# Transposing by VectorE blocks and a detour through DRAM in a two-layer attention kernel

## The chip, the cores and the metric

The kernel runs on one core of one Trainium2 chip. The core has five engines that run side by side, each with its own queue of instructions: TensorE (PE, matrix products; PEld is its weight load), VectorE (DVE), ScalarE (ACT), GpSimd (POOL) and SyncE (SP), which in this kernel issues every DMA. An engine takes its instructions strictly in the order the build has given it, and waits on semaphores for what other engines or DMAs deliver. The metric is the time of one launch on the device in microseconds, as the median of several runs; beside it stands one profiled execution with a trace of every instruction.

## What is computed

Four images of 128 channels and 64 x 64 pixels (4096 tokens) go through two layers. The reference, cut to what matters:

```python
# layer 0, channels first
g = _gn(x)                                            # group norm
v, gate = split(sigmoid(conv_bn(g, Wvg, svg, bvg)))
q = conv_bn(g, Wq, sq, bq) * 64**-0.5; k = conv_bn(g, Wk, sk, bk)
attn = softmax(q.T @ k)
x = x + conv_bn((v @ attn.T) * gate, Wp, sp, bp)
# layer 1, tokens first
t = to_tokens(x)
h = _ln_t(t); q = h @ W1
t = t + softmax(q @ q.T) @ h                          # symmetric scores
f = batch_norm(_ln_t(t) @ W2.T)
t = t + scan over tokens of y = sigmoid(f_t + y @ V.T)
x = from_tokens(t, x)
```

All data is 32-bit float. Layer 0 works with channels on the 128 partitions, the layer norms need tokens on the partitions, and the products after them need channels again. So tiles of 128 x 512 are turned over several times for each block of 512 tokens.

## The kernel before

Each image is handled alone, in a loop over `b`: group norm (`group_norm`), the projections q, k, v and gate (`project`), attention of layer 0 (`layer0`), attention of layer 1 (`layer1`). After the fourth image comes the token scan.

**Layer 0.** Eight blocks `n` of 512 queries. For each block 16 pairs of key tiles: two score products into `ps` (L186), the exponential on ScalarE into one of five buffers `e` (L189), the running sum of `e` on VectorE (`acc`, L198), and the weighted sums `o` (L326). When a block is done, `finish` puts five steps into the list `pending`, and the loop takes one of them out after every second pair of the next block, so that they fall between the products of that block: `sums` (the denominators), `residual` (four transposes of the input `xb` by TensorE, L351, and a copy on ScalarE), `tokens` (the output projection straight into token order, four products of 128 columns, L357; the sum with the residual; layer norm into `h`), `turn` (four transposes of `h` by TensorE, L372, and a copy), `queries` (the product with layer 1's weight into `qt`, L377). The steps of the last block have no next block to hide in: `flush` runs them one after the other, and layer 1 begins with the `qt` that they make.

**Layer 1.** The scores are symmetric, so only the blocks (n, a) with a <= n are computed (L502, exponential L508). Each tile `e` with a < n is used twice: as it is (`direct`, L404), and turned over (`reversed_products`, L417). To turn it over, VectorE transposes it in 32 x 32 blocks into `dd` (L513), and 16 DMAs of 64 KB move the blocks to where they belong in `tt` (L532), SBUF to SBUF. There are 28 such turned tiles for each image, two buffers `dd` and three buffers `tt`; a turned tile is due four steps of the loop after it was made. The row sums of a turned tile are taken by VectorE (L422) and its product is added to `oacc` (L429). When the last turned tile of a block is done, `finish` puts four steps into `pending`: `tokens` (four transposes of `oacc` by TensorE, L456, sum with `t`, layer norm into `h2`), `result` (four transposes of `t`, L467, a copy, one store of 256 KB to `t2_d`, L470), `turn` (four transposes of `h2`, L475, a copy into `th`), `inputs` (the product `mw`, L480, its statistics, and a copy into `wxs`). Blocks run from n = 7 down to 0, so the blocks get shorter towards the end of an image, and the steps of the last blocks fall into the next image's `project`, or after the fourth image into a bare `flush`.

A step's work is written into the code at the place where it is taken out of `pending`; the build then orders the instructions of each engine's queue, and this order is fixed when the kernel runs. SP's queue holds the loads of `x`, the stores and loads of `t_d`, the 16 DMAs of each turned tile and the stores of the result, all in one line: an entry that waits holds everything behind it.

Of the kernel before, what the change touches and what calls it, by code (L numbers as in the profile page):

```python
# [9 lines left out]
F32 = mybir.dt.float32  # L10
# [7 lines left out]
P = 128  # L18
B, C, N = 4, 128, 4096
# [3 lines left out]
NT = N // P  # L23
# [5 lines left out]
QB = 512  # L29
NB = N // QB  # L30
NQ = QB // P
# [17 lines left out]
def conv_attn_hybrid_kernel(  # L49
# [8 lines left out]
    nc = tc.nc  # L58
# [5 lines left out]
    t_d = dram.tile([B, NB, P, NQ, C], F32, name="t_d")  # L64
# [43 lines left out]
    def inv_sqrt(dst, var, eps):  # L108
# [6 lines left out]
        tc, x, out, t_d, t2_d,  # L115
# [21 lines left out]
def fast(  # L137
    tc, x, out, t_d, t2_d, wt, col, par, bpc, bc, ident, gavg, ones, shift, inv_sqrt, par_ok
):
    nc = tc.nc  # L140
# [7 lines left out]
    with ExitStack() as st:  # L148
# [10 lines left out]
        pending: deque = deque()  # L159

# [60 lines left out]

        def layernorm(src, dst):

            mv = stat.tile([P, NQ, 2], F32, tag="mv", name="mv")
            rstd = stat.tile([P, NQ], F32, tag="rstd", name="rstd")
            for j in range(NQ):
                s6 = stat.tile([P, 6], F32, tag="s6", name="s6")
                nc.vector.bn_stats(s6, src[:, j, :])  # L228
                nc.vector.bn_aggr(mv[:, j, :], s6)  # L229
            inv_sqrt(rstd, mv[:, :, 1], EPS_LN)  # L230
            for j in range(NQ):
                nc.vector.tensor_scalar(  # L232
                    dst[:, j, :], src[:, j, :], mv[:, j, 0:1], rstd[:, j : j + 1],
                    ALU.subtract, ALU.mult,
                )

# [74 lines left out]
        def layer0(b, gate, q, k, v):  # L311
# [20 lines left out]
            def finish(n, o, acc):  # L332
                cs, ts = bass.ts(n, QB), bass.ts(n, NQ)
                og = work.tile([P, QB], F32, tag="og", name="og")
                nc.scalar.copy(og, o[1])
                nc.vector.tensor_tensor(og, o[0], og, ALU.add)
                nc.vector.tensor_tensor(og, og, gate[:, cs], ALU.mult)
                rinv = stat.tile([P, NQ], F32, tag="rinv", name="rinv")
                xb = work.tile([P, QB], F32, tag="xb", name="xb", bufs=2)
                t = work.tile([P, NQ, C], F32, tag="t", name="t", bufs=2)  # L340
                ht = work.tile([P, QB], F32, tag="th", name="ht")
                nc.sync.dma_start(xb, x[b, :, cs])
                nc.gpsimd.tensor_scalar(xb, xb, bpc, None, ALU.add)  # L343

                def sums():
                    denominators(acc, b * NT + n * NQ, rinv)

                def residual():
                    m = ps_m.tile([P, NQ, P], F32, tag="m", name="mx")
                    for j in range(NQ):  # L350
                        nc.tensor.transpose(m[:, j, :], xb[:, bass.ts(j, P)], ident)  # L351
                    nc.scalar.copy(t, m)

                def tokens():
                    m = ps_m.tile([P, NQ, P], F32, tag="m", name="mt")
                    for j in range(NQ):
                        nc.tensor.matmul(  # L357
                            m[:, j, :], lhsT=og[:, bass.ts(j, P)], rhs=wt["ps"],
                            start=True, stop=True,
                        )  # L360
                    for j in range(NQ):
                        nc.vector.scalar_tensor_tensor(
                            t[:, j, :], m[:, j, :], rinv[:, j : j + 1], t[:, j, :],
                            ALU.mult, ALU.add,
                        )
                    nc.sync.dma_start(t_d[b, n], t)
                    layernorm(t, h[:, ts, :])

                def turn():
                    m = ps_m.tile([P, QB], F32, tag="m", name="mh")  # L370
                    for j in range(NQ):
                        nc.tensor.transpose(m[:, bass.ts(j, P)], h[:, n * NQ + j, :], ident)  # L372
                    nc.scalar.copy(ht, m)

                def queries():
                    m = ps_m.tile([P, QB], F32, tag="m", name="mq")
                    nc.tensor.matmul(m, lhsT=wt["a"], rhs=ht, start=True, stop=True)  # L377
# [7 lines left out]
        def layer1(b, h, qt):  # L385
# [55 lines left out]
            def finish(n):  # L441
                cs = bass.ts(n, QB)
                rinv = stat.tile([P, NQ], F32, tag="rinv", name="rinv")
                t = work.tile([P, NQ, C], F32, tag="t", name="t1", bufs=2)
                h2 = work.tile([P, NQ, C], F32, tag="h2", name="h2")
                th = work.tile([P, QB], F32, tag="th", name="th")
                nc.sync.dma_start(t, t_d[b, n])

                def tokens():
# [4 lines left out]
                    m = ps_m.tile([P, NQ, P], F32, tag="m", name="mt")  # L454
                    for j in range(NQ):
                        nc.tensor.transpose(m[:, j, :], oacc[:, n, bass.ts(j, P)], ident)  # L456
# [5 lines left out]
                    layernorm(t, h2)  # L462

                def result():
                    m = ps_m.tile([P, QB], F32, tag="m", name="mr")
                    for j in range(NQ):
                        nc.tensor.transpose(m[:, bass.ts(j, P)], t[:, j, :], ident)  # L467
                    t2 = work.tile([P, QB], F32, tag="xb", name="t2", bufs=2)
                    nc.scalar.copy(t2, m)
                    nc.sync.dma_start(t2_d[b, :, cs], t2)  # L470

                def turn():
                    m = ps_m.tile([P, QB], F32, tag="m", name="mh")
                    for j in range(NQ):
                        nc.tensor.transpose(m[:, bass.ts(j, P)], h2[:, j, :], ident)  # L475
                    nc.scalar.copy(th, m)

                def inputs():
                    m = ps_m.tile([P, QB], F32, tag="m", name="mw")
                    nc.tensor.matmul(m, lhsT=wt["f"], rhs=th, start=True, stop=True)  # L480
# [6 lines left out]
                pending.extend([tokens, result, turn, inputs])  # L487

            for n in range(NB - 1, -1, -1):
                o = None  # L490
                for a in range(n, -1, -1):
# [37 lines left out]
                    if a < n:  # L529
                        for p in range(NQ):  # L530
                            for f in range(NQ):
                                nc.sync.dma_start(  # L532
                                    t[bass.ts(f, 32), p], d[bass.ts(p, 32), f]
                                )
                        turned.append((clock + 4, n, a, t))
# [14 lines left out]
        ok = stat.tile([P, 2, 2 * B * NT], F32, tag="ok", name="ok", bufs=1)  # L550
# [490 lines left out]
```

## Time and profile before

| | us |
|---|---|
| median of 3 runs | 3354.91 (3354.78 to 3356.2) |
| the profiled execution, its own time | 3355.76 |
| its span, first to last instruction | 3353.9 |

| row of the profile | busy us | one takes, ns |
|---|---|---|
| PE, layer 0 products `o` (L326) | 960.1 | 590 |
| PE, layer 0 scores `ps` (L186) | 539.5 | 608 |
| PE, layer 1 scores (L502) | 547.3 | 604 |
| PE, layer 1 direct products (L404) | 527.7 | 592 |
| PE, layer 1 turned products (L417) | 402.8 | 592 |
| ACT, layer 0 exponential (L189) | 521.0 | 1024 |
| ACT, layer 1 exponential (L508) | 391.2 | 683 |
| DVE, layer 0 running sums (L198) | 548.7 | 1225 |
| DVE, row sums of turned tiles (L422) | 252.9 | 2258 |

A row gives the code line, the engine, the instruction, output and input. Matrix instructions overlap in the pipeline, so busy time divided by the count is less than the duration of one. A 32-bit product appears as two instructions, a transpose as one. The granted TensorE clock was 0.972 over the span. DMA engines moved 179.24 MB, 53 GB/s in the mean.

### The profile page before, as it was taken

The page shows a single profiled execution, that of the slowest core. Times are in us where ns is not written, and L with a number is a line of the kernel's source. Part 1 is how long each engine was busy: PE and PEld are TensorE (multiplying, and loading weights), DVE is VectorE, ACT ScalarE, POOL GpSimd, SP SyncE. Part 2 cuts the span into 40 slices and gives each one's busy share as a digit, 9 for nine tenths or more (in the row PEclk, how much of TensorE's full clock was granted, in tenths as well). Part 3 has the DMA queues.
Part 4 walks back from the last instruction along what each step waited for, and adds up shares of the span by engine and source line. Part 5 has one row for each costly group of instructions (what it writes and reads, how often), then busy time and mean ns, then how long its engine had stood idle before and what let it go on. Part 6 is the DMA issues. An engine that isn't in the chain of part 4 may idle for free.

```text
span 3353.9 us, 32409 instructions
## 1 busy us (share of the span) xinstructions
PE 3148.9 (94%) x11210; PEld 1437.9 (43%) x11210; DVE 1708.3 (51%) x2793; ACT 1171.5 (35%) x2050; POOL 144.1 (4%) x183
## 2 busy tenths in 40 slices
PE   6999999997899999999699999999979999999976
PEld 3444444443444444444344444444434444444433
DVE  4545544555555544555645554455555555345556
ACT  3443432332434333233244343323233444332324
POOL 0000000000000000000000000000000000000000
PEclk9999999998999999999899999999989999999998
DMA  1000023332000003333200001333300000233334
GB/s 41 13 10 10 10 70 90 92 91 88 10 10 13 13 13 88 91 90 92 67 7 13 13 7 35 90 95 93 102 26 13 7 13 10 63 91 92 91 97 175
DMA packets 109084, 179.24 MB, mean 53 GB/s; under 512 B 31472, under 2 KB 31984, under 8 KB 107888
## 3 DMA queue, kind: packets, MB, share of 16 engines
q1 hardware_dynamic: 108912, 177.08, 19.4%
q8 instruction: 92, 1.51, 0.2%
q14 instruction: 80, 0.66, 0.1%
HBM read 34.35 MB, written 25.17 MB: 18 GB/s over the span
## 4 chain that ended last, share of the span: by engine, by line
PE 88%; DVE 6%; ACT 2%; POOL 1%; issue 1%; DMA 1%; SPq 0%; DVEq 0%; POOLq 0%; ACTq 0%
PE o L326 26%; PE ps L186 14%; PE ps L502 14%; PE o L404 14%; PE ot L417 11%; PE mq L377 1%; PE pvg L293 1%; PE mt L357 1%; POOL rstd L111 1%; PE md L214 1%; PE mw L480 1%; PE pvg L297 1%; DMA xg<-in_x_dram 1%; DVE t L458 1%; DVE s L228 1%
## 5 line engine op out<-in xcount | busy, mean ns | idle before, releaser
L326 PE MATMUL o<-e,v 64*128 64x512 f32 x4096 | 960.1, 590 | 0.0
L198 DVE TENSOR_TENSOR acc<-acc,e 128x1024 f32<-128x1024 f32 x448 | 548.7, 1225 | 525.3 <-ACT e L189 519.5
L189 ACT ACTIVATE e<-ps 128x1024 f32<-128x1024 f32 x512 | 521.0, 1024 | 684.5 <-PE ps L186 684.5
L508 ACT ACTIVATE e<-ps,shift 128x512 f32<-128x512 f32 x576 | 391.2, 683 | 940.1 <-PE ps L502 768.3
L326 PEld LDWEIGHTS o<-e,v 64*128 64x128 f32 x4096 | 397.3, 188 | 486.6 <-issue 479.0
L502 PE MATMUL ps<-qt 128*128 128x512 f32 x1152 | 547.3, 604 | 2.7 <-ACT qt L378 2.7
L186 PE MATMUL ps<-q,k 64*128 64x512 f32 x2048 | 539.5, 608 | 9.0 <-ACT e L189 4.8
L404 PE MATMUL o<-e,h 128*128 128x512 f32 x1152 | 527.7, 592 | 0.0
L417 PE MATMUL ot<-tt,h 128*128 128x512 f32 x896 | 402.8, 592 | 0.0
L513 DVE STREAM_TRANSPOSE dd<-e 128x512 f32<-128x512 f32 x448 | 285.7, 683 | 125.1 <-ACT e L508 82.4
L502 PEld LDWEIGHTS ps<-qt 128*128 128x128 f32 x1152 | 217.6, 194 | 269.9 <-issue 240.0
L404 PEld LDWEIGHTS o<-e,h 128*128 128x128 f32 x1152 | 217.1, 191 | 260.2 <-issue 260.2
L186 PEld LDWEIGHTS ps<-q,k 64*128 64x128 f32 x2048 | 185.6, 187 | 223.1 <-issue 123.2
L417 PEld LDWEIGHTS ot<-tt,h 128*128 128x128 f32 x896 | 170.2, 190 | 214.3 <-issue 212.4
L422 DVE TENSOR_REDUCE slots<-tt 128x4 f32<-128x2048 f32 x112 | 252.9, 2258 | 2.3 <-DMA tt<-dd 1.7
L429 DVE TENSOR_TENSOR oacc<-oacc,ot 128x512 f32<-128x512 f32 x84 | 57.4, 684 | 309.7 <-PE ot L417 309.7
L232 DVE TENSOR_SCALAR h<-t,mv,rstd 128x128 f32<-128x128 f32 x256 | 73.0, 346 | 94.5 <-POOL rstd L111 94.4
L508 ACT ACTIVATION_READ_ACCUMULATOR e<-ps,shift 128x1 f32 x576 | 113.0, 196 | 0.0
L343 POOL TENSOR_SCALAR xb<-xb,bpc 128x512 f32<-128x512 f32 x32 | 57.0, 1781 | 1112.4 <-DMA xb<-in_x_dram 1112.4
L110 POOL TENSOR_SCALAR rstd<-mv 128x4 f32<-128x4 f32 x64 | 14.6, 229 | 1949.0 <-DVE mv L229 1949.0
L427 DVE COPY oacc<-ot 128x512 f32<-128x512 f32 x28 | 19.4, 692 | 139.5 <-PE ot L417 139.5
L293 PE MATMUL pvg<-w_vs,xg 128*128 128x128 f32 x256 | 42.7, 318 | 31.9 <-ACT xg L304 23.8
(112 smaller groups left out, 1510.9 us busy)
## 6 DMA issues: line engine op xcount, KB each, us to landing
tt<-dd SPq DMA_DIRECT2D x1792, 64.0 KB, 2.0
t_d<-t SPq DMA_DIRECT2D x64, 256.0 KB, 2.0
xg<-in_x_dram SPq DMA_DIRECT2D x16, 512.0 KB, 5.6
xb<-in_x_dram SPq DMA_DIRECT2D x32, 256.0 KB, 2.7
t<-t_d SPq DMA_DIRECT2D x32, 256.0 KB, 2.7
t2s<-t_d SPq DMA_DIRECT2D x4, 2048.0 KB, 14.8
out_dram<-t2s SPq DMA_DIRECT2D x4, 2048.0 KB, 15.6
w<-in_wts_dram SPq DMA_DIRECT2D x1, 512.0 KB, 3.5
```

The costliest lines, as they stand in the source:

```text
L186: nc.tensor.matmul(ps[:, h, :], lhsT=lhsT, rhs=rhs, start=True, stop=True)
L189: nc.scalar.activation(e, ps, AF.Exp, scale=scale)
L198: nc.vector.tensor_tensor(acc, acc, e, ALU.add)
L232: nc.vector.tensor_scalar(dst[:, j, :], src[:, j, :], mv[:, j, 0:1], rstd[:, j : j + 1], ALU.subtract, ALU.mult,)
L293: nc.tensor.matmul(pv[:, 0, bass.ts(i, P)], lhsT=xg[:, bass.ts(4 * ch + i, P)], rhs=wt["vs"], start=True, stop=True,)
L326: nc.tensor.matmul(o[r], lhsT=v[rs, p + h * PAIRS, :], rhs=e[rs, h, :], start=(p == 0 and h == 0), stop=(p == PAIRS - 1 and h == 1),)
L404: nc.tensor.matmul(o, lhsT=h[:, NQ * a + 2 * i + half, :], rhs=e[:, half, :], start=(a == n and i == 0 and half == 0), stop=(a == 0 and i ...
L417: nc.tensor.matmul(ot, lhsT=h[:, NQ * n + j, :], rhs=t[:, :, j, :, :].rearrange("q p k j -> q k p j"), start=(j == 0), stop=(j == NQ - 1),)
L422: nc.vector.tensor_reduce(slots[:, bass.ts(n, NQ), a], t.rearrange("q p b k j -> q b p (k j)"), AX.XY, ALU.add,)
L502: nc.tensor.matmul(ps[:, half, :], lhsT=qt[:, bass.ts(at, P)], rhs=qt[:, bass.ts(n, QB)], start=True, stop=True,)
L508: nc.scalar.activation(e[:, half, :], ps[:, half, :], AF.Exp, bias=shift, accum_out=slots[:, at, n : n + 1],)
L513: nc.vector.transpose(d.rearrange("q f b k j -> q k b f j")[:, 2 * i + half], e[:, half, :].rearrange("q (b f j) -> q b f j", b=NQ, f=NQ),)
```

## The change

All transposes by TensorE go. A new helper `move` takes their place: VectorE transposes a 128 x 512 tile in 32 x 32 blocks into a tile `d` (two buffers), one DMA of 256 KB writes `d` to a scratch tensor in DRAM (`turn0_d` to `turn7_d` in turn), and four DMAs of 64 KB, one for each group of 32 partitions, read it back in the wanted order. The five DMAs all go through SP's queue, and the four that read wait there until the one that writes has landed.

- Layer 0: `residual` and `turn` are gone. `sums` moves `xb` to `t`; the new step `projection` makes one product of 512 columns with `w_ps` as the stationary operand, in channel order, and moves it to `yt`; `tokens` adds, stores, normalises and moves `h` to `ht`. Empty steps (`nothing`) hold `tokens` and `queries` two places after the step before them.
- Layer 1: `weighted` moves `oacc` to `ot`; `tokens` adds, transposes `t` in blocks and stores it straight to the result in `t2_d` with 16 DMAs of 16 KB (runs of 32 numbers), normalises, and moves `h2` to `th`; `inputs` is as before.
- The turned tiles of layer 1 go the same way: one DMA of 1 MB to `tiles0_d` to `tiles3_d`, and four of 256 KB back, in place of 16 of 64 KB.
- `xb` has one buffer in place of two; `t`, `ot`, `th` have a layout in four groups of 32 tokens, and `ok` lies in another pool.

```diff
-    t_d = dram.tile([B, NB, P, NQ, C], F32, name="t_d")
+    t_d = dram.tile([B, NB, P, 4, NQ, 32], F32, name="t_d")
+    tiles_d = [dram.tile([P, NQ, NQ, NQ, 32], F32, name=f"tiles{i}_d") for i in range(4)]
+    turn_d = [dram.tile([P, 4, NQ, 32], F32, name=f"turn{i}_d") for i in range(8)]
...
+        def move(blocks, dst):
+            nonlocal n_moves
+            d = work.tile([P, 4, NQ, 32], F32, tag="d", name="d", bufs=2)
+            nc.vector.transpose(d.rearrange("q a j i -> q j a i"), blocks)
+            via = turn_d[n_moves % len(turn_d)]
+            n_moves += 1
+            nc.sync.dma_start(via, d)
+            for a in range(4):
+                nc.sync.dma_start(dst[bass.ts(a, 32)], via[:, a].rearrange("(p i) j k -> i p j k", p=4))
...
 # layer 0, finish
                 def sums():
                     denominators(acc, b * NT + n * NQ, rinv)
-                def residual():
-                    m = ps_m.tile([P, NQ, P], F32, tag="m", name="mx")
-                    for j in range(NQ):
-                        nc.tensor.transpose(m[:, j, :], xb[:, bass.ts(j, P)], ident)
-                    nc.scalar.copy(t, m)
+                    move(xb.rearrange("c (j f k) -> c j f k", j=NQ, f=4), t)
+                def projection():
+                    m = ps_m.tile([P, QB], F32, tag="m", name="mt")
+                    nc.tensor.matmul(m, lhsT=wt["ps"], rhs=og, start=True, stop=True)
+                    move(m.rearrange("c (j f k) -> c j f k", j=NQ, f=4), yt)
                 def tokens():
-                    m = ps_m.tile([P, NQ, P], F32, tag="m", name="mt")
-                    for j in range(NQ):
-                        nc.tensor.matmul(
-                            m[:, j, :], lhsT=og[:, bass.ts(j, P)], rhs=wt["ps"],
-                            start=True, stop=True,
-                        )
                     for j in range(NQ):
                         nc.vector.scalar_tensor_tensor(
-                            t[:, j, :], m[:, j, :], rinv[:, j : j + 1], t[:, j, :],
+                            t[:, :, j, :], yt[:, :, j, :], rinv[:, j : j + 1], t[:, :, j, :],
                             ALU.mult, ALU.add,
                         )
                     nc.sync.dma_start(t_d[b, n], t)
-                    layernorm(t, h[:, ts, :])
-                def turn():
...
+                    layernorm(tiles(t), quarters(h[:, ts, :]))
+                    move(h[:, ts, :].rearrange("q j (p i) -> q j p i", p=4), ht)
...
-                pending.extend([sums, residual, tokens, turn, queries])
+                pending.extend([sums, projection, nothing, tokens, nothing, queries])
...
 # layer 1, finish
+                def weighted():
...
+                    move(oacc[:, n, :].rearrange("c (j f k) -> c j f k", j=NQ, f=4), ot)
+                def tokens():
                     for j in range(NQ):
                         nc.vector.scalar_tensor_tensor(
-                            t[:, j, :], m[:, j, :], rinv[:, j : j + 1], t[:, j, :],
+                            t[:, :, j, :], ot[:, :, j, :], rinv[:, j : j + 1], t[:, :, j, :],
                             ALU.mult, ALU.add,
                         )
...
+                    d = work.tile([P, 4, NQ, 32], F32, tag="d", name="d", bufs=2)
+                    nc.vector.transpose(d.rearrange("q p j k -> q j p k"), t.rearrange("q p j i -> q j p i"))
+                    to = t2_d[b, :, cs].rearrange("(p i) (j f k) -> f i p j k", p=4, f=4, j=NQ)
+                    for f in range(4):
+                        for p in range(4):
+                            nc.sync.dma_start(to[f, :, p], d[bass.ts(f, 32), p])
+                    layernorm(tiles(t), quarters(h2))
+                    move(h2.rearrange("q j (p i) -> q j p i", p=4), th)
...
-                pending.extend([tokens, result, turn, inputs])
+                pending.extend([weighted, nothing, tokens, nothing, inputs])
...
 # layer 1, turned tiles
-                        for p in range(NQ):
-                            for f in range(NQ):
-                                nc.sync.dma_start(
-                                    t[bass.ts(f, 32), p], d[bass.ts(p, 32), f]
-                                )
+                        via = tiles_d[n_turned % len(tiles_d)]
+                        nc.sync.dma_start(via, d)
+                        for f in range(NQ):
+                            nc.sync.dma_start(
+                                t[bass.ts(f, 32)], via[:, f].rearrange("(p i) b k j -> i p b k j", p=4)
+                            )
```

More of the change, by code (lines that the diff above doesn't have):

```diff
@@ L137, in fast @@
 def fast(
-    tc, x, out, t_d, t2_d, wt, col, par, bpc, bc, ident, gavg, ones, shift, inv_sqrt, par_ok
+    tc, x, out, t_d, t2_d, turn_d, tiles_d, wt, col, par, bpc, bc, ident, gavg, ones, shift, inv_sqrt, par_ok
 ):
@@ L159, in fast, with nothing @@
         pending: deque = deque()
+        def nothing():
+            pass
         def flush():
@@ L232, in layernorm, with tiles, quarters @@
                 nc.vector.tensor_scalar(
-                    dst[:, j, :], src[:, j, :], mv[:, j, 0:1], rstd[:, j : j + 1],
+                    dst[j], src[j], mv[:, j, 0:1], rstd[:, j : j + 1],
                     ALU.subtract, ALU.mult,
                 )
+        def tiles(t):
+            return [t[:, :, j, :] for j in range(NQ)]
+        def quarters(t):
+            return [t[:, j, :].rearrange("q (p i) -> q p i", p=4) for j in range(NQ)]
         def group_norm(b):
@@ L460, in tokens @@
                             ALU.mult, ALU.add,
                         )
[L462 to L470, printed above, removed]
```

40 lines of the change are left out of this document (17 added, 23 removed).

## Prediction

> **What bounds the kernel now.** I read the busy shares and the chain of waits first, then the time by stage, then single timelines.
>
> ```profile
> PE 3148.9 (94%) x11210; PEld 1437.9 (43%) x11210; DVE 1708.3 (51%) x2793; ACT 1171.5 (35%) x2050; POOL 144.1 (4%) x183
> PE 88%; DVE 6%; ACT 2%; POOL 1%; issue 1%; DMA 1%; SPq 0%; DVEq 0%; POOLq 0%; ACTq 0%
> ```
>
> TensorE is busy 94% and 88% of the chain is its work. The stages of one image (start:end, length, PE busy, ...) show where it is not:
>
> ```profile
> 60.00:426.00 366.00, 366.00 (x1712) 166.30 (x1708) 186.80 (x268) 144.81 (x156) 19.72 (x20) 1.00 0.03 10
> 426.00:439.00 13.00, 6.20 (x27) 3.65 (x28) 4.97 (x20) 2.30 (x4) 1.27 (x2) 0.68 0.19 62
> 439.00:802.00 363.00, 360.21 (x878) 160.38 (x878) 180.25 (x295) 110.51 (x299) 7.60 (x12) 0.99 0.36 90
> ...
> 3240.00:3265.00 25.00, 13.74 (x46) 7.23 (x44) 14.34 (x45) 2.35 (x4) 2.64 (x5) 0.77 0.10 30
> ```
>
> Layer 0 (366 us) and layer 1 (363 us) are TensorE from end to end: work taken from it there is time won. Between them lie 13 us, a chain of dependent steps with nothing beside it, four times; the fourth row is the same kind of chain at the end of the last image. There each added step is time lost. So the change is a trade: TensorE time in the long stages against latency in the short ones, and against whatever lands too late in the long ones.
>
> **What leaves TensorE.** In layer 0 four transposes sit between a pair's products (PE timeline: start, length):
>
> ```profile
> 196.99 1.88 PE L326 MATMUL o<-e,v 64*128 64x512 f32 x8
> 198.80 0.66 PE L351 MATMUL mx<-ident,xb 128*128 128x128 f32 x4
> ...
> 200.35 1.88 PE L326 MATMUL o<-e,v 64*128 64x512 f32 x8
> ...
> 202.93 1.88 PE L326 MATMUL o<-e,v 64*128 64x512 f32 x8
> ```
>
> A pair with them takes 3.36 us, the next without 2.58: 0.79 for four transposes, with the change between row layouts. A block has two such groups (L351, L372); the projection stays as dear (four products of 128 columns, 1.29 by the same reading; one of 512 like L377, 1.26). Seven of eight blocks lie under products: 2 x 0.79 x 7 x 4 = **-44 us**. In layer 1:
>
> ```profile
> 789.08 0.60 PE L456 MATMUL mt<-ident,oacc 128*128 128x128 f32 x4
> 789.52 1.88 PE L502 MATMUL ps<-qt 128*128 128x512 f32 x4
> ```
>
> 0.44 per group, three groups per block, five blocks (n = 7 to 3) whose steps fall inside the stage: 3 x 0.44 x 5 x 4 = **-26 us**. The copies leave ScalarE, which is never full. VectorE gains three block transposes per block, 683 ns each by row L513, 192 in all, 131 us; at 187 of 366 and 180 of 363 us it has room, so they cost only where something waits for them.
>
> **The price of a move.** Rows of the DMA list and of SP's timeline:
>
> ```profile
> tt<-dd SPq DMA_DIRECT2D x1792, 64.0 KB, 2.0
> t_d<-t SPq DMA_DIRECT2D x64, 256.0 KB, 2.0
> ...
> 452.68 17.68 SPq L532 DMA_DIRECT2D tt<-dd  x28
> ```
>
> A store of 256 KB lands 2.0 us after issue; one of 64 KB on 32 partitions too, and SP spends 17.68 / 28 = 0.63 on each. A move is 0.68 (VectorE) + 2.0 (store; SP waits) + 3 x 0.63 (issues before the last) + 2.0 = 6.6, with hand-overs 6.9. The bounds of an issue: 0.32 (t_d in the timeline below) and, where the longer pattern is dearer, 1.2 (my doubling of 0.63; no row has it). I take 0.63, since the new DMAs are on 32 partitions as those are.
>
> **The gap between the layers.**
>
> ```profile
> 428.76 1.13 PE L357 MATMUL mt<-w_ps,og 128*128 128x128 f32 x8 [0.89 <-DVE og L337]
> 429.98 1.13 DVE L362 SCALAR_TENSOR_TENSOR t<-mt,rinv,t 128x128 f32<-128x128 f32 x4 [1.37 <-PE mt L357]
> 431.17 0.32 SPq L366 DMA_DIRECT2D t_d<-t  x1
> ...
> 433.70 1.11 DVE L232 TENSOR_SCALAR h<-t,mv,rstd 128x128 f32<-128x128 f32 x4 [1.47 <-POOL rstd L111]
> 434.11 1.24 PE L372 MATMUL mh<-ident,h 128*128 128x128 f32 x4 [4.22 <-DVE h L232]
> 435.38 0.59 ACT L373 COPY ht<-mh 128x512 f32<-128x512 f32 x1 [6.89 <-PE mh L372]
> ```
>
> Between product and sum goes a whole move, +6.9, and a 512-column product that runs cold (2.07 for `mq` a little later, against 1.13), about +0.5; from `h` to `ht` 1.9 becomes 6.9, +5.0. That is 12.4, four times **+50 us** (issue 0.32: +42; 1.2: about +64). The move of `xb` is issued long before and stays hidden.
>
> [...]
>
> **Layer 0, is the rest covered?** From the start of `mt`: product 1.2, block transpose done 2.0, `yt` landed 8.1, sum and layer norm 4.83 (429.98 to 434.81) 13.0, block transpose 13.8, `ht` landed 20.1. In the changed order `mq` stands eight pairs behind `mt`: 1.29 + 8 x 2.574 = 21.9. Cover 1.8 us, cost 0. If each of the two moves takes 1 us more it is gone, and each us beyond costs 28. Behind the sum on VectorE wait the `acc` additions of some three pairs; with five buffers `e` this holds.
>
> **Layer 1, what lands late.** Turned tiles: out 1 MB, by the four 2 MB stores at the end (24.3 us for 8 MB: 3.0 per MB, plus 1.3 latency) 4.3; back 1.9 + 2 to 3. SP is held 0.4 + 4.3 + 2.5 per tile, less than 16 x 0.63 = 10.1 before; product wanted some 20 us after the transposes. Covered by itself. But SP now also has, for each block, the store and loads of `ot`, 16 result stores (16 x 0.63 = 10.1), and store and loads of `th`, in line with the tiles. I followed the fixed order, TensorE at 0.86 per 512-column product. Block 4, counted from the first score of block 3: VectorE stands behind the turned product that ends at 48.0, then `oacc` 0.7, four block transposes 2.8, sum and its transpose 2.2: result ready 53.7, its stores issued until 63.3, `th` stored and landed 65.7, loaded 70.0. TensorE is at `mw` at 65.3: 5 us late. Block 3: ready 92, stored 102, `th` there at 108, TensorE at `mw` at 102 (7 late), and the last turned tile, queued behind the same stores, 2 more. Block 5 the same way 2 + 2. Block 6: VectorE waits for a turned product before it frees an `e` that a score needs, 4.7. Block 7: 1. Sum 24 per image, **+95 us**. With issues at 0.43 (128-partition loads, 1.76 / 4 at 802) it is 12 per image, 51; at 0.32 nothing. Price if all is doubled: 190.
>
> **Image borders and the end.** The blocks 2 to 0 finish inside the next `project`: `mw` of block 1 comes some 4 us late by the same chain, layer norm of block 2 shares VectorE with the group norm, 2: 6 x 3 = **+18** (0 to 36). After the last image three blocks run bare: 26, then 18 per block for 10.1 of stores, two moves and the norm, about 62 us where 23 were, **+39** (20 to 60).
>
> **Sum.** -44 - 26 + 50 + 95 + 18 + 39 = +132. The profiled execution had 3355.8, so 3488; its like lies 0.9 over the median: **3487 us**, 3.9% slower.
>
> **Rivals.**
> - *Faster: everything in the long stages is covered.* Place: SP's queue in layer 1. It decides if an issue takes 0.32 or less: then the stores of block 4 end at 58.8 and `th` lands before 65.3. For it: t_d's row. Against: 28 issues in a line at 0.63. Then -44 - 26 + 42 + 0 + 0 + 20 = -8, and `project` (57 us, TensorE busy 39) may give back the transposes and copies of three blocks, up to 7 us at three borders: 3326 to 3347, say 3335.
> - *The short runs are dear.* At 1.2 per result store SP holds 9 us more in each finish: five late blocks become 3 x 9 x 4 = 108 more, borders and end some 50, gaps 14: about 3660. For it: no row has runs of 128 bytes. Against: 128 runs of 2 KB issue in 0.32.
> - *Layer 0 stalls too.* One us more per move ends its cover of 1.8 and costs about 28: 3515, inside the range.
> - *No change*: gains and losses cancel between the first rival and the forecast.
>
> **Numbers.** Forecast 0.59, layer 0 too 0.14, dear runs 0.10, faster 0.14, no change 0.03. A difference under 0.2% (7 us) can't be told from none. Slower 0.83, same 0.03, faster 0.14. The likeliest case by itself runs from 3420 (issue 0.43) to 3580 (late landings doubled); the range leaves out the faster rival and most of the dear one: 3385 to 3600.
>
> **What would show it.** Right: the gap between layers near 25 us; SP issues of result stores near 0.6 in unbroken lines of 16; PE idle before `mw` waiting for a DMA of `th`; layer 0 at about 355 us; the stretch after the last turned product near 60. Wrong: no wait of `mw` on a DMA, or layer 1 shorter than 360; or waits at `mq` in layer 0; or VectorE, not SP, named as what releases `th` late.

## The result, and the profile after

| | before | after |
|---|---|---|
| median of the runs, us | 3355.25 (4 runs) | 3500.76 (4 runs, 3498.33 to 3502.22) |
| ratio | | 1.0433, 95% interval 1.0415 to 1.0451 |
| span of the profiled execution, us | 3353.9 | 3499.0 |
| granted TensorE clock | 0.972 | 0.944 |

The change makes the kernel 4.3% slower. The busy shares and the chain of waits of the changed kernel:

```profile
PE 3077.4 (88%) x10378; PEld 1358.1 (39%) x10378; DVE 1845.7 (53%) x2985; ACT 1096.0 (31%) x1922; POOL 144.6 (4%) x183
...
PE 73%; DMA 10%; DVE 7%; SPq 6%; issue 2%; ACT 2%; POOL 0%; DVEq 0%; ACTq 0%; POOLq 0%
```

TensorE has 832 instructions and 71.5 us of busy time less, as the change means it to. But its share of the chain falls from 88% to 73%. DMA (10%, before 1%) and SP's queue (6%, before 0%) have come into it: TensorE is often no longer what ends last.

The stages of the first image (start:end, length, busy time of PE, PEld, DVE, ACT, POOL with counts, granted clock, DMA share, GB/s):

```profile
58.00:413.00 355.00, 354.34 (x1616) 157.38 (x1616) 200.25 (x289) 138.35 (x143) 21.87 (x21) 1.00 0.13 42
413.00:438.00 25.00, 4.75 (x12) 1.79 (x12) 6.42 (x22) 0.91 (x2) 1.26 (x2) 0.56 0.22 74
438.00:827.00 389.00, 362.70 (x810) 155.97 (x809) 192.66 (x300) 105.23 (x289) 6.34 (x10) 0.96 0.63 173
```

Layer 0 is 11 us shorter and still all TensorE. The gap between the layers is 25 us in place of 13. Layer 1 is 389 us in place of 363, although it has 68 matrix instructions fewer: TensorE is busy 362.7 of 389, and the clock is 0.96 in place of 0.99. Bytes pass at nearly twice the rate in that stage (173 GB/s against 90).

What TensorE waits for, over the whole run (waiting tile and line, what it waits for: us in total, times, longest):

```profile
PE mq L395 <- DMA ht<-turn_d: 70.8, 4, 17.7
PE ot L437 <- DMA tt<-tiles_d: 70.2, 16, 5.4
PE mw L494 <- DMA th<-turn_d: 58.9, 11, 16.5
...
PE ps L518 <- ACT e L524: 21.2, 12, 4.3
```

The first row is the gap, four times 17.7 us; in a timeline of TensorE (start, length, instruction, idle time before it and what ended it):

```profile
415.54 1.62 PE L380 MATMUL mt<-og,w_ps 128*128 128x512 f32 x2 [1.86 <-DVE og L365]
434.87 2.05 PE L395 MATMUL mq<-ht,w 128*128 128x512 f32 x2 [17.71 <-DMA ht<-turn_d]
437.59 2.93 PE L518 MATMUL ps<-qt 128*128 128x512 f32 x3 [0.68 <-ACT qt L398]
```

The second and fourth rows are inside layer 1. Of the third, 7.1 us are inside layer 1; the rest falls at the image borders and the end. What a turned tile meets in SP's queue is seen in SP's timeline (the profile leaves out buffer numbers, so the result tensor `t2_d` appears as `t_d`):

```profile
633.77 7.43 SPq L488 DMA_DIRECT2D t_d<-d  x16
641.29 0.38 SPq L237 DMA_DIRECT2D turn_d<-d  x1
641.72 0.43 SPq L547 DMA_DIRECT2D tiles_d<-dd  x1
643.36 2.51 SPq L239 DMA_DIRECT2D th<-turn_d  x4
646.20 1.73 SPq L549 DMA_DIRECT2D tt<-tiles_d  x4
```

The 16 result stores hold SP for 7.43 us. Only behind them go the store of `h2` for `th` and the store of a turned tile (L547), which had nothing to do with the result. That tile still comes in time. In the next block one does not; it is the 21st of the 28, matched by order (VectorE, then SP, then TensorE):

```profile
685.40 1.38 DVE L529 STREAM_TRANSPOSE dd<-e 128x512 f32<-128x512 f32 x2 [2.34 <-ACT e L524]
700.18 0.70 DVE L484 STREAM_TRANSPOSE d<-t 128x512 f32<-128x512 f32 x1
700.91 7.46 SPq L488 DMA_DIRECT2D t_d<-d  x16
708.89 0.43 SPq L547 DMA_DIRECT2D tiles_d<-dd  x1
713.38 1.73 SPq L549 DMA_DIRECT2D tt<-tiles_d  x4
721.51 6.19 PE L437 MATMUL ot<-tt,h 128*128 128x512 f32 x8 [5.02 <-DMA tt<-tiles_d]
```

The tile is ready at 686.78 and its store goes out at 708.89, 22.1 us later. For the first 14.1 of them SP issues nothing: the entry at its head, the first result store, waits for the transposition of `t`, which VectorE ends at 700.88. The other 8.0 are the issues of the 16 stores and of the store for `th`. So the tile is held by the place behind a waiting entry as well as by the number of stores.

### The profile page after: what moved, and what is told of

The parts are those of the page before. It is cut to its first block, busy times and chain, and to the rows that moved or that the text cites. A ratio compares the mean times of both kernels' runs of the same rounds, so it can differ in the third digit from the quotient of the medians.

```text
span 3499.0 us, 31099 instructions
## 1 busy us (share of the span) xinstructions
PE 3077.4 (88%) x10378; PEld 1358.1 (39%) x10378; DVE 1845.7 (53%) x2985; ACT 1096.0 (31%) x1922; POOL 144.6 (4%) x183
## 4 chain that ended last, share of the span: by engine, by line
PE 73%; DMA 10%; DVE 7%; SPq 6%; issue 2%; ACT 2%; POOL 0%; DVEq 0%; ACTq 0%; POOLq 0%
PE o L354 25%; PE ps L192 13%; PE o L424 11%; PE ps L518 9%; PE ot L437 8%; DMA tiles_d<-dd 4%; SPq L488 4%; DMA tt<-tiles_d 3%; PE mq L395 1%; PE mt L380 1%; DVE dd L529 1%; PE md L220 1%; PE pvg L321 1%; SPq L549 1%; DVE t L479 1%
## 5 line engine op out<-in xcount | busy, mean ns | idle before, releaser
L518 PE MATMUL ps<-qt 128*128 128x512 f32 x1152 | 545.9, 610 | 23.9 <-ACT e L524 21.2
L192 PE MATMUL ps<-q,k 64*128 64x512 f32 x2048 | 530.0, 599 | 6.5 <-ACT e L195 4.8
L437 PE MATMUL ot<-tt,h 128*128 128x512 f32 x896 | 429.5, 627 | 70.2 <-DMA tt<-tiles_d 70.2
L437 PEld LDWEIGHTS ot<-tt,h 128*128 128x128 f32 x896 | 179.4, 202 | 306.5 <-issue 275.3
L395 PE MATMUL mq<-ht,w 128*128 128x512 f32 x64 | 39.7, 705 | 70.8 <-DMA ht<-turn_d 70.8
L494 PE MATMUL mw<-th,w 128*128 128x512 f32 x64 | 42.8, 757 | 59.2 <-DMA th<-turn_d 58.9
```

Source lines behind the costliest of these rows:

```text
L192: nc.tensor.matmul(ps[:, h, :], lhsT=lhsT, rhs=rhs, start=True, stop=True)
L437: nc.tensor.matmul(ot, lhsT=h[:, NQ * n + j, :], rhs=t[:, :, j, :, :].rearrange("q p k j -> q k p j"), start=(j == 0), stop=(j == NQ - 1),)
L518: nc.tensor.matmul(ps[:, half, :], lhsT=qt[:, bass.ts(at, P)], rhs=qt[:, bass.ts(n, QB)], start=True, stop=True,)
```

## The experiments

Theory at the start: the gain in layer 0 is real; the loss is the latency of the detour where nothing covers it (gap, end), and in layer 1 the finish steps and their 16 stores standing in one queue with the turned tiles. Rivals for layer 1: the tiles' way through DRAM lands too late; the doubled DMA traffic slows everything.

For layer 1, one account was made of every run from the records of the matrix instructions, from the first score to the last turned product of an image. "Waits" are the gaps between the end of one and the start of the next. "Slow products" is the time by which 512-column products of more than 0.62 us exceed 0.60. "Rest" is the length less these two. Mean of four images, us:

| kernel | time of the run | layer 1 | waits | slow products | rest |
|---|---|---|---|---|---|
| before | 3355.3 | 364.1 | 3.0 | 3.6 | 357.5 |
| turned tiles by DRAM only | 3354.7 | 364.5 | 3.5 | 3.4 | 357.6 |
| layer 1's steps by moves only | 3502.8 | 386.7 | 25.9 | 12.4 | 348.4 |
| the changed kernel | 3500.8 | 386.9 | 24.7 | 13.6 | 348.6 |
| 16 stores of a quarter size | 3494.1 | 385.0 | 23.7 | 12.7 | 348.6 |
| four stores | 3424.4 | 373.3 | 14.6 | 10.3 | 348.4 |
| result by TensorE, one store | 3415.4 | 374.7 | 13.6 | 10.6 | 350.5 |
| four stores, finish DMAs on GpSimd | 3452.4 | 379.9 | 20.8 | 10.8 | 348.3 |
| 16 stores on ScalarE | 3540.3 | 401.9 | 34.2 | 19.6 | 348.1 |
| 16 stores behind the move of `h2` | 3578.6 | 411.4 | 47.5 | 15.4 | 348.5 |
| tiles on ScalarE | 3595.1 | 420.8 | 55.7 | 16.9 | 348.3 |

### Turned tiles by DRAM alone

```diff
 (kernel before)
-                        for p in range(NQ):
-                            for f in range(NQ):
-                                nc.sync.dma_start(t[bass.ts(f, 32), p], d[bass.ts(p, 32), f])
+                        via = tiles_d[n_turned % len(tiles_d)]
+                        nc.sync.dma_start(via, d)
+                        for f in range(NQ):
+                            nc.sync.dma_start(
+                                t[bass.ts(f, 32)], via[:, f].rearrange("(p i) b k j -> i p b k j", p=4))
```

> The kernel before with one part of the change alone: layer 1's turned exponential tiles go by one 1 MB store to DRAM and four 256 KB loads, where before 16 DMAs went from SBUF to SBUF. Main theory (the loss in layer 1 is the finish steps, their 16 result stores and the moves standing in SP's one queue; the tiles alone are read four steps after they are written and stay covered): about 3355 us, within 10 us of before, and TensorE's wait of ot for tt does not grow by more than 5 us per image. Rival (the tile's way by DRAM, 5.5 us for the store and 6.2 for a load in the profile after, is what layer 1 waits for): +60 to +100 us, 3415 to 3455.

3354.68 us, ratio 0.9996 (0.9987 to 1.0006). This part costs nothing. Its DMA row and queue row:

```profile
q1 hardware_dynamic: 103536, 294.44, 31.3%
...
tiles_d<-dd SPq DMA_DIRECT2D x112, 1024.0 KB, 5.1
```

The tiles bring the traffic from 177 to 294 MB and take 5.1 us for their store, and layer 1 stays at 364.5 us. So neither the traffic of the tiles nor their longer way is by itself what layer 1 waits for.

### Layer 0 alone

```diff
 (kernel before)
-                pending.extend([sums, residual, tokens, turn, queries])
+                if by_pe(n):
+                    pending.extend([sums, residual, tokens, turn, queries])
+                else:
+                    pending.extend([sums, projection, nothing, tokens_moved, nothing, queries])
```

Here `by_pe` holds for no block. `sums`, `projection`, `tokens_moved` and `queries` do what the change does in layer 0.

> The kernel before with layer 0's steps by moves for all eight blocks of an image, layer 1 and its tiles as before. Main theory: -45 us of TensorE work in the blocks whose moves lie under the next block, +48 us in the four gaps between the layers, where three moves in a row lie under nothing, so about 3358 us (3345 to 3370). Rival (the moves of layer 0 also slow what runs beside them, by DMA traffic or clock): above 3380 us. Rival (TensorE loses as much in the gap as before and layer 0 is a plain gain): about 3312 us.

3355.55 us, ratio 1.0002 (0.9992 to 1.0012). From the last `o` product to layer 1's first score 24.8 to 25.1 us pass (before 12.9), so four gaps lose some 48 us. A block under products takes 44.90 us in place of 46.50, which wins 45 us over 28 blocks. Gain and loss cancel, as worked out.

### Layer 0 in the hidden blocks only

```diff
 (the kernel of the last experiment)
         def by_pe(n):
-            return False
+            return n == NB - 1
```

Blocks for which `by_pe` holds keep the old steps: `residual`, `tokens`, `turn`, `queries` with TensorE's transposes.

> The kernel before with layer 0's steps by moves in the blocks 0 to 6 of an image alone; the last block, whose steps nothing covers, keeps its TensorE transposes, and so does all of layer 1. Main theory: the -45 us remain and the gap stays at its old 12.9 us, so about 3310 us, faster than both kernels. Rival (the gain of layer 0 is tied to the gap, for instance because a step taken off TensorE only lets its clock or its waits grow): 3345 to 3360 us.

3310.04 us, ratio 0.9864 (0.9842 to 0.9886): 1.4% faster than the kernel before, and faster than both. The gap is 12.9 to 13.8 us. The trade is won by taking the move only where other work covers it.

### The changed kernel with the gap by TensorE

```diff
 (changed kernel)
-                pending.extend([sums, projection, nothing, tokens, nothing, queries])
+                if n == NB - 1:
+                    pending.extend([sums, residual, product, turn, queries])
+                else:
+                    pending.extend([sums, projection, nothing, tokens, nothing, queries])
```

`residual`, `product` and `turn` are the four transposes, the four products in token order and the four transposes of before.

> The changed kernel with the steps of layer 0's last block done again by TensorE; all else as changed. Main theory: each of the four gaps between the layers falls from 24.8 to about 13 us, -48 us in all, so about 3452 us (3440 to 3465). Rival (the gap is long because layer 1's start waits for something else as well, such as queues full of the moves of earlier blocks): less than 20 us gained, above 3480 us.

3455.39 us, ratio 1.0304 (1.0287 to 1.0321): 45.4 us less than the changed kernel; the gaps are 12.9 to 13.8 us. The gap's price is the way by moves: with TensorE's transposes in the last block it goes, all else being as changed.

### Layer 1's steps alone

```diff
 (kernel before)
-                pending.extend([tokens, result, turn, inputs])
+                pending.extend([weighted, nothing, tokens, nothing, inputs])
```

The steps are those of the change, the 16 stores included; the turned tiles keep their old 16 DMAs.

> The kernel before with layer 1's finish steps by moves and its result by 16 stores per block; its turned tiles keep their 16 DMAs each, layer 0 is as before. Main theory (the steps and stores in SP's one queue are the cause, and the tile's way by DRAM even lightens that queue, from 16 DMAs to 5 per tile): the gaps between the layers stay short, but layer 1 loses at least what it lost in the changed kernel, about +100, and the end of the kernel its +33; with SP's 28 x 16 tile DMAs still there, 3490 to 3560 us. Rival (layer 1's loss needs both the tile's DRAM traffic and the steps, by full DMA engines): the steps alone cost less than half, 3355 to 3430 us.

3502.78 us, ratio 1.0443 (1.0425 to 1.0460). The steps by themselves cost all that the whole change costs, at 98 GB/s in the first image's layer 1 (before 90, changed 173). So the loss does not need the doubled DMA traffic; the rival of full DMA engines falls as its cause. One detail of the expectation is not borne out: five DMAs per tile in place of 16 show no relief in layer 1 (386.9 against 386.7). Whether a shorter line at SP and the greater traffic offset each other there is not shown.

### The result by TensorE and one store

```diff
 (changed kernel)
-                    d = work.tile(...)
-                    nc.vector.transpose(d..., t...)
-                    for f in range(4):
-                        for p in range(4):
-                            nc.sync.dma_start(to[f, :, p], d[bass.ts(f, 32), p])
...
+                def result():
+                    m = ps_m.tile([P, QB], F32, tag="m", name="mr")
+                    for j in range(NQ):
+                        nc.tensor.transpose(m[:, bass.ts(j, P)], tn[:, j, :], ident)
+                    t2 = work.tile([P, QB], F32, tag="og", name="t2")
+                    nc.scalar.copy(t2, m)
+                    nc.sync.dma_start(t2_d[b, :, cs], t2)
```

> The changed kernel, but layer 1's result is turned by four TensorE transposes per block, copied by ScalarE and stored with one 256 KB DMA, in place of VectorE's turning and 16 stores. Price on TensorE: 0.79 us x 32 blocks = +25 us. Main theory (the 16 stores hold SP for 7.6 us per block, and with them th, whose 58.9 us of waiting by mw is the largest part of layer 1's loss beside the tiles): mw's wait falls under 30 us and the tiles' waits fall with it; 3440 us (3415 to 3470). Rival (the tile's landing or full DMA engines set layer 1, not the queue): the 25 us come on top, 3500 to 3530 us.

3415.42 us, ratio 1.0176 (1.0159 to 1.0193), 85 us less than the changed kernel, though TensorE has 128 transposes more. In layer 1 the waits fall from 24.7 to 13.6 us per image. `ot`'s wait for `tt` falls from 70.2 to 18.9 us over the run; `mw`'s, expected under 30, only from 58.9 to 47.6.

### Is it the number or the size of the stores?

```diff
 (changed kernel, 16 stores with a quarter of the bytes)
-                            nc.sync.dma_start(to[f, :, p], d[bass.ts(f, 32), p])
+                            nc.sync.dma_start(to[f, :, p, 0], d[bass.ts(f, 32), p, 0])
...
 (changed kernel, four stores)
+    tb_d = dram.tile([B, C, 4, NB, P], F32, name="tb_d")
...
-                        for p in range(4):
-                            nc.sync.dma_start(to[f, :, p], d[bass.ts(f, 32), p])
+                        nc.sync.dma_start(to[f], d[bass.ts(f, 32)].rearrange("i p j k -> i p (j k)"))
```

> The changed kernel with the same 16 result stores per block, each with a quarter of its bytes and of its 128-byte runs (the first 128 of 512 tokens; the rest of layer 1's result is not stored, and the final sum takes the input in its place). If the number of DMAs in SP's queue is the cost (7.6 us for 16, whatever they carry): no more than 10 us faster, 3488 to 3505. If the many short runs are the cost, in SP's issue or in the DMA engines: layer 1 falls by 8 us or more per image, 3400 to 3460.

> The changed kernel with 4 result stores of 64 KB per block in place of 16 of 16 KB, into a scratch tensor in an order of its own, and four loads per image in place of one when the result is read at the end; VectorE's turning stays, TensorE gets nothing back. If the number of stores in SP's queue is the cost: the gain of the kernel with the result by TensorE (85 us) plus the 25 us that its transposes cost there, so about 3390 us (3375 to 3420), layer 1 at 366 to 372 us. If that gain came from VectorE, which lost its fourth transposition there: little here, 3460 to 3500 us.

A quarter of the bytes (this kernel leaves three quarters of layer 1's result unstored): 3494.08 us, ratio 1.0414 (1.0397 to 1.0431), 7 us less than the changed kernel. Four stores: 3424.42 us, ratio 1.0210 (1.0193 to 1.0227), 76 us less. SP's timeline of the quarter-size kernel, and its DMA list (count, KB each, median us from issue to landing):

```profile
636.19 7.29 SPq L488 DMA_DIRECT2D t_d<-d  x16
```

```profile
t_d<-d SPq DMA_DIRECT2D x512, 4.0 KB, 1.4
```

and SP's timeline of the kernel with four stores, at the same block as the first SP lines shown above (633.77 on):

```profile
633.29 1.76 SPq L488 DMA_DIRECT2D tb_d<-d  x4
637.53 0.34 SPq L238 DMA_DIRECT2D turn_d<-d  x1
637.92 0.43 SPq L547 DMA_DIRECT2D tiles_d<-dd  x1
```

16 stores take 7.29 us with 4 KB each and 7.43 us with 16 KB each: SP's time is paid per DMA here. The count matters far more than the bytes: a quarter of the bytes saves 7 us, four stores in place of 16 save 76. With four, the turned tile's store goes out at 637.92 in place of 641.72. The gain was 76 and not the 110 us that I expected: layer 1 gives back 13.6 of the 22.8 us per image that it lost and keeps 14.6 us of waits, and the end keeps 141.2 us after the last turned product, where the result by TensorE has 134.0, the changed kernel 146.3 and the kernel before 111.5. The number of stores is the largest single cause in layer 1, not the only one: the 21st tile is still held 19.5 us (ready at 681.08, stored at 700.58), since the entries ahead of it still wait for VectorE.

### The stores moved behind the move of h2

```diff
 (changed kernel)
-                    (the 16 stores)
                     layernorm(tiles(t), quarters(h2))
                     move(h2.rearrange("q j (p i) -> q j p i", p=4), th)
+                    (the 16 stores)
```

> The changed kernel with the 16 result stores of each block of layer 1 written behind the move of h2 instead of ahead of it; number and size of the DMAs stay. If only the place of the stores matters (th queued behind them): the three bare blocks after the last image save some 7 us each, mw's waits go, and the total comes down by 30 to 60 us, 3440 to 3470. If what matters is that SP is held for 7.6 us per block wherever the stores stand, because the next turned tile waits there too: only the end gains, some 15 to 20 us, and layer 1 stays at 384 to 389 us, 3475 to 3495. I hold the second for likelier, since ot's wait for tt (70.2 us) is now larger than mw's in layer 1 (7.1 us inside the stage).

3578.56 us, ratio 1.0671 (1.0653 to 1.0688), 78 us more than the changed kernel: both expectations fell. TensorE's longest wait, and then a stretch of SP's timeline:

```profile
PE ot L437 <- DMA tt<-tiles_d: 146.3, 17, 16.4
```

```profile
713.65 0.34 SPq L237 DMA_DIRECT2D turn_d<-d  x1
714.04 1.88 SPq L490 DMA_DIRECT2D t_d<-d  x4
716.01 1.80 SPq L239 DMA_DIRECT2D th<-turn_d  x4
717.85 5.66 SPq L490 DMA_DIRECT2D t_d<-d  x12
723.56 0.90 SPq L547 DMA_DIRECT2D tiles_d<-dd  x2
```

SP issues nothing from 690.8 to 713.65, because the entry at its head is the store of `h2`'s transposition, which VectorE finishes at 713.62. VectorE had finished one turned tile at 686.31 and the next at 706.94; their stores go out at 723.56, behind everything of the finish step, and `ot` stands still for 16.25 us for the first of them. In the changed kernel the tile's store stands ahead of the loads of `th`. The edit also makes the build order other instructions anew, so the 78 us are not the price of the place alone; but the rows show the same mechanism as the 16 stores, an entry that waits at the head and a finished tile behind it.

### Other queues

> The changed kernel with the 16 result stores of each block of layer 1 issued by ScalarE instead of SP. Main theory (SP is held for 7.6 us per block by them, and th and the next tile behind them are late): mw's wait for th falls by half or more, the end of the kernel by some 7 us per block that ends there, 3440 us (3410 to 3465). Rival (ScalarE's exponentials stand behind the stores just as SP's tiles did): the wait moves to the scores, 3490 to 3530 us.

> The changed kernel with the five DMAs of each turned tile issued by ScalarE instead of SP. Main theory (tiles and finish steps stand in each other's way in SP's one queue): ot's 70.2 us of waiting for tt and mw's waits both fall, 3420 us (3400 to 3460), unless ScalarE's own exponentials now stand behind a DMA that waits. Rival (the tile's landing itself is too slow, or the DMA engines are too full): ot's wait for tt stays above 50 us, 3480 us or more.

```diff
 (changed kernel, 16 stores on ScalarE)
-                            nc.sync.dma_start(to[f, :, p], d[bass.ts(f, 32), p])
+                            nc.scalar.dma_start(to[f, :, p], d[bass.ts(f, 32), p])
...
 (changed kernel, tiles on ScalarE; the four loads likewise)
-                        nc.sync.dma_start(via, d)
+                        nc.scalar.dma_start(via, d)
```

3540.29 us, ratio 1.0553 (1.0536 to 1.0571), and 3595.09 us, ratio 1.0710 (1.0692 to 1.0728): both worse. The first is what its rival said, though longer than its 3490 to 3530 us; the second is the exception that its main theory named, far beyond its range. ScalarE's timeline with the stores, and then with the tiles:

```profile
642.74 7.32 ACTq L488 DMA_DIRECT2D t_d<-d  x14
650.11 0.69 ACT L524 ACTIVATE e<-ps,shift 128x512 f32<-128x512 f32 x1 [7.49 <-DMA t_d<-d]
```

```profile
619.82 8.46 ACTq L549 DMA_DIRECT2D tt<-tiles_d  x4
628.38 0.69 ACT L524 ACTIVATE e<-ps,shift 128x512 f32<-128x512 f32 x1 [8.61 <-DMA t_d<-d]
```

An exponential now stands 7.5 or 8.6 us behind DMAs in ScalarE's own queue, and TensorE needs that exponential: with the stores there, the scores wait 61.3 us for `e` where 21.2 were. ScalarE is busy only 31% of the span, but what it does is wanted at once. With the tiles there, `ot`'s wait is gone as hoped, and `mw`'s wait for `th` is 242.7 us, by far the longest; why `th` comes so late there stays open.

> The changed kernel with four result stores (as in the run with four stores, 3424 us), and all DMAs of layer 1's finish steps (the two moves and the stores) issued by GpSimd, which is 4% busy; only the turned tiles, the loads and layer 0's moves stay with SP. If it is one queue that ties tiles and finish steps together: ot's wait for tt falls under 10 us over the whole run, layer 1 comes to 364 to 368 us per image, the total to 3395 (3385 to 3410). If GpSimd is held by a DMA that waits, or its DMAs are dearer, so that th or rstd comes late: the wait moves to mw, and the time is 3424 us or more.

```diff
 (kernel with four stores; the move of h2 likewise)
-                    move(oacc[:, n, :].rearrange("c (j f k) -> c j f k", j=NQ, f=4), ot)
+                    move(oacc[:, n, :].rearrange("c (j f k) -> c j f k", j=NQ, f=4), ot, nc.gpsimd)
...
-                        nc.sync.dma_start(to[f], d[bass.ts(f, 32)].rearrange("i p j k -> i p (j k)"))
+                        nc.gpsimd.dma_start(to[f], d[bass.ts(f, 32)].rearrange("i p j k -> i p (j k)"))
```

3452.35 us, ratio 1.0297 (1.0272 to 1.0321), 28 us more than with SP alone. TensorE's longest wait, and then GpSimd's timeline:

```profile
PE mw L494 <- DMA th<-turn_d: 121.4, 22, 22.6
```

```profile
688.95 2.17 POOL L488 DMA_DIRECT2D tb_d<-d  x4 [31.73 <-DVE d L485]
691.26 0.23 POOL L114 TENSOR_SCALAR rstd<-mv 128x4 f32<-128x4 f32 x1
...
694.80 0.64 POOL L238 DMA_DIRECT2D turn_d<-d  x1 [2.19 <-DVE d L235]
699.82 2.18 POOL L240 DMA_DIRECT2D th<-turn_d  x4 [4.39 <-issue]
```

One half of the theory held: each of the 112 tile stores goes out within 0.1 us of VectorE's end, and `ot` does not wait for a tile any more, in no image, where with the same four stores on SP it waits 26.1 us. So it was the common queue that made tiles late. The other half fell: the stores now stand ahead of `rstd`, a step of the layer norm that GpSimd computes, a move's store takes 3.1 us to land in place of 2.0, and `mw` waits 83 us inside layer 1 where 9.8 were. How these two divide the 83 us is not shown.

## Why the prediction came out as it did

The prediction said 3487 us, the measurement 3501, within the range. The trade it described is what happened; that the sum comes so near is partly luck. Its terms, in us over the whole run (measured from the span's parts, before to after):

| term | predicted | measured | from |
|---|---|---|---|
| layer 0's TensorE work | -44 | -45 | a block from 46.50 to 44.90 us, x 7 x 4 |
| layer 1's TensorE work | -26 | -36 | "rest" 357.5 to 348.6, x 4 |
| gaps | +50 | +46 | 12.9 to 24.5, x 4 |
| layer 1, waits | +95 | +87 | 3.0 to 24.7, x 4 |
| layer 1, slow products | no term | +40 | 3.6 to 13.6, x 4 |
| image borders | +18 | +19 | last turned product to next first score 449.0 to 455.9, less 0.5 for layer 0 and gap, x 3 |
| end | +39 | +35 | 111.5 to 146.3 |
| sum | +132 | +146 | spans: +145 |

*Layer 0 and the gap*: right in mechanism and size, and shown three times (layer 0 alone, hidden blocks only, the gap by TensorE). No wait of `mq` appeared inside the blocks, so the cover of 1.8 us held. A move in the gap took 6.3 us (417.20 to 423.53) and not 6.9. Against that, the sum counted 1.9 us for what a move replaces behind `h`, from the first transposition on; from the end of `h` it is 1.2 (434.81 to 435.97).

*Layer 1's TensorE work.* In each image 68 transposes lay inside the stage, 17 groups of four and not 15. At the 0.44 us of the prediction that is 30 of the 36 us; the rest is not accounted for.

*A missing term.* The prediction counted TensorE's waits in layer 1 but not what a wait costs afterwards. It had that effect in the gap ("a 512-column product that runs cold") and left it out of layer 1. Eight turned products in the changed kernel, without a wait and after one (TensorE's timeline):

```profile
585.11 3.60 PE L437 MATMUL ot<-tt,h 128*128 128x512 f32 x8
...
794.44 5.37 PE L437 MATMUL ot<-tt,h 128*128 128x512 f32 x8 [3.49 <-DMA tt<-tiles_d]
```

1.77 us more for the same eight. Over the run this is +40 us, the largest error of the sum. A layer-1 TensorE term too small by 10 and waits, gaps and end too large by 16 offset part of it.

*The waits of layer 1: the size by luck, the place wrong.* For each image the prediction put 14 us of waits at `mw`, 4 at turned products, 4.7 at scores that need an `e`, and 1 in block 7. Inside layer 1 of the changed kernel they are 1.8 at `mw`, 17.6 at turned products and 5.3 at scores (over the run 7.1, 70.2 and 21.2 of 98.7). So two wrong sizes offset each other.

`mw` was put too late: an issue takes 0.46 us (7.43 / 16) and not 0.63, and `th` is there 13.8 us after the result is turned, not 16.3. In the block shown above it lands at 714.66, and `mw` starts at 715.47 without a wait. The turned product behind `mw`, at 721.51, is the one that waits.

The tiles were put too early: "covered by itself", and 2 us late behind the stores in two blocks, while the store above is held 22.1 us. Their loads are slower too: 8.0 us from the first issue to the last landing (713.38 to 721.38), where 1.9 and 2 to 3 were taken; that store's 4.4 is as assumed.

By the prediction's own alternative of 0.43 per issue the waits would be 51 us in all; they are 87. How much of the difference the slower loads make is not shown: with the tiles on their old way and layer 1's steps alone, the waits are as long (25.9 us per image). The DMA list of the changed kernel:

```profile
tiles_d<-dd SPq DMA_DIRECT2D x112, 1024.0 KB, 5.5
tt<-tiles_d SPq DMA_DIRECT2D x448, 256.0 KB, 6.2
turn_d<-d SPq DMA_DIRECT2D x160, 256.0 KB, 2.0
...
t_d<-d SPq DMA_DIRECT2D x512, 16.0 KB, 1.5
```

In the run with tiles by DRAM alone, landings like these (5.1 us for a tile's store) were covered; behind the finish step's entries they are not.

The cause is the one named, the finish step's DMAs in SP's line; the victim is another. The wait in block 6 for an `e` that VectorE frees late was foreseen with 4.7 us and took 4.13.

*The rivals.* Dear short runs fell: a store of 16 KB in 128-byte runs lands in 1.5 us, and a quarter of the runs saves 7 us in all. "Everything in the long stages is covered" holds for layer 0 and the tiles, not for layer 1's steps.

With four stores 14.6 us of waits per image remain in layer 1, 58.4 over the run: 26.1 of `ot` for a tile, 8.4 of `ot` for VectorE, 14.1 of scores for an `e`, 9.8 of `mw` for `th`. Open is what another order of VectorE's work would take from them. A layer 1 that moves only some blocks was not tried.

## What to carry to other kernels

Cost a detour by latency, not by work: the same move gave 45 us where a block of other work lay over it and took 46 where nothing did, and choosing it block by block beat both kernels (3310 us). Count the DMAs that a step issues and ask what else stands in that queue: here 16 small stores, 7.4 us of a queue per block, and an entry at its head that waited 14 us for VectorE made unrelated tiles late, and carrying the stores to an engine whose own results are wanted soon made it worse (on ScalarE 3540 us). A stall of the engine that sets the end is worth more than its length when the clock falls with it: here 87 us more of waits in layer 1 brought 40 us of slower products.

## What the runs showed of the hardware

- *Waits and the clock.* In layer 1 of the first image of the changed kernel, the waits of 0.32, 0.82, 0.98 and 1.69 us leave the next products at 0.59 to 0.70 us; the five of 3.49 to 5.40 us are each followed by three to six products of 0.9 to 1.2 us. In between, the length does not decide alone: waits of 3.16 and 3.27 us in its second and fourth image left the next products at 0.59 to 0.67 us, and the wait of 1.9 us ahead of `mt`, the same in all four gaps, left its two instructions at 0.67 and 0.59 us in three images and at 0.77 and 1.06 us in the first (415.54 on, shown above as one of 1.62). The granted clock in the traces of both kernels is 1.0 or 0.5 and changes only at points that lie multiples of 3.41 us apart. In the first image it falls to 0.5 at 415.98, within `mt`; in the others it falls 0.03 to 0.15 us behind `mt`'s end. So it seems to matter also where a wait falls.
- *An issue has a price of its own here.* SP takes 0.46 us for each store of 4 KB and of 16 KB alike and 0.44 for one of 64 KB (1.76 / 4), ScalarE 0.52 (7.32 / 14), GpSimd 0.54 (2.17 / 4).
- *Short runs are not dear here.* 128-byte runs to DRAM, 512 DMAs of 16 KB, land in 1.5 us by the median, stores of a quarter of that in 1.4; a store of 256 KB lands in 2.0 and those of 64 KB with longer runs in 1.8.
